# A sandwich layer on one core: where the expert mixing runs, how its chunks are paired, and where T4 is kept

## The chip, the cores and the metric

The kernel runs on one core of a Trainium2 chip. The metric is the device time of one execution in microseconds (us), the median of several runs. The core has a matrix engine (TensorE, PE in the profile, with its weight loads as PEld), VectorE (DVE), ScalarE (ACT), GpSimd (POOL) and SyncE (SP), whose queue issues all the DMA transfers of this kernel. Each engine takes its own instructions in the order in which the program emits them, and waits on semaphores for the others.

## The reference

Windowed attention with a residual, and then a feed-forward layer whose weights are mixed for each batch out of a base and eight experts, with a gate:

```python
x = x + layernorm(attention(layernorm(x), w_qkv))      # (4, 2048, 512), 16 heads, windows of 128
x = x + layernorm(ffn(layernorm(x), ...))

def ffn(hidden_states, ...):                            # (4, 2048, 512)
    h = relu(einsum('bsh,oh->bso', x, gate_w1) + gate_b1)
    g = (einsum('bso,eo->bse', h, gate_w2) + gate_b2).mean(axis=1)   # 8 numbers per batch
    mW1 = W1 + einsum('be,efh->bfh', g, TW1)            # 2048 x 512 per batch
    mb1 = b1 + g @ Tb1
    mW2 = W2 + einsum('be,ehf->bhf', g, TW2)            # 512 x 2048 per batch
    mb2 = b2 + g @ Tb2
    u = gelu(einsum('bsh,bfh->bsf', x, mW1) + mb1[:, None, :])
    return einsum('bsf,bhf->bsh', u, mW2) + mb2[:, None, :]
```

The gate's mean runs over a sequence's 2048 tokens, so each of the four sequences (the kernel's batches) has its own eight numbers and its own mixed weights. All is in float32.

## The kernel before

**Two phases.** First attention for all 64 windows, as a loop over 256 slots (`for i in range(NS)`, four slots to a window, one for each group of four heads). Into the slots lists of functions put the other work: norms, projections, the gate's products, the output. Then the feed-forward layer, as a loop over 16 blocks of 512 tokens (`for K in range(NBK)`), four blocks to a batch, so blocks 0 to 3 belong to batch 0 and blocks 8 to 11 to batch 2.

**Matrix products in Strassen's manner.** The products are cut into 2 x 2 quarters and done with seven products in place of eight (Winograd's form), for which sums of quarters of the left and the right factor are needed. The names A11, A12, S1 to S4, A22 are the seven left factors, T1 to T4 the sums of the right factor. For the second layer of batches 2 and 3 (`DEEP`, blocks 8 to 15) this is done twice, one inside the other: seven outer products (`o` from 0 to 6), each out of seven inner ones, with inner sums of the left factor (the weights) made once per batch and inner sums of the right factor (the activations) made by `inner_sums` for each block.

**A block.** Its first layer is four sets of two chunks (`for c in range(0, HC, 2)`), each of seven products: `begin` emits two, `middle` four, and the last one (A22, into the bank X) is emitted by `end` inside the next set's `middle`, or inside the second layer for the last set. In `middle` DVE adds Z into the tile `cpb` (L1145) and X into the tile `cpv` (L1148); the last product of the set writes X and so waits for L1148. Between its products `middle` calls `step()` four times, which advances the mixing. The second layer is `second` for batches 0 and 1 and `second_deep` for 2 and 3. Its weights come through `load_second`, from a list of all the tiles of all blocks (`coming`), into six buffers: six tiles are loaded ahead, and whenever PE has finished with a tile the next of the list is loaded. So the last tiles' places of a block take the first six of the next block.

**The mixing.** `mixer` is a generator over a list of jobs (`todo`). "mix" loads one expert's chunk (128 x 1024, 512 KB, into `exps`, four buffers) and adds it, times the gate's number, to `acc` on DVE (L251). A job can have two batches, and then one load serves two such additions. "sum" makes the three sums of a chunk and a difference (L262 to L265, in the tile `sums`, one buffer; on POOL while attention runs, then on DVE) and has the result stored into the weights' place in memory (`m1d`, `m2d`, `m3d`). "inner" loads two stored chunk pairs of batch 2, makes the inner sums (L117 to L120, on DVE) and stores them. Loads are three jobs ahead; stores are kept in `late` and issued by `flush` at the next job. A "mix" gives control back after each batch, an "inner" after each job, and a "sum" only in the feed-forward phase. For batch 3 the accumulators lie where the gate's weights were, so they can't begin until the gate is over, which is in block 0's second layer.

The list runs: batches 0 and 1 with both layers, chunk by chunk; chunks 0 to 3 of batch 2's first layer; the second layer of batches 2 and 3 in pairs; chunks 4 to 7 of the first layer in pairs, with inner sums of batch 2 behind each; chunks 0 to 3 of batch 3's first layer alone, with the rest of batch 2's inner sums. That is 416 expert loads and 512 additions. `MIXED` says how many steps each attention slot takes from slot 85 on (25 in 16 slots), `mixing(...)` how many are taken at each of the four calls in `middle` and after each of the seven products in `second`. The first list must have ended by block 8's second layer. The fourteen inner sums of batch 3 are a generator of their own (`inner_mixer`), stepped in block 9's first layer, with loads two ahead.

**T4 in the deep second layer.** T1 is used in the outer product 1, T3 in 3 (it lies in `top[..., Q:]`), T4 in 6. T4 is made by four subtractions on POOL (L1409), in T1's place, emitted in products 3 and 4.

Of the kernel before, what the change touches and what calls it, by code (L numbers as in the profile page):

```python
# [11 lines left out]
ALU = mybir.AluOpType  # L12
# [5 lines left out]
NB, L, D = 4, 2048, 512  # L18
# [6 lines left out]
NBLK = L // TB  # L25
# [9 lines left out]
def sandwich(ctx: ExitStack, tc: tile.TileContext, x, w_qkv, gw1, gb1, gw2, gb2, w1, b1, w2, b2, tw1, tb1, tw2, tb2, out):  # L35
# [72 lines left out]
    def load_inner(b, o, h):  # L108
        two = slice(2 * h, 2 * h + 2)
        et = mix.tile([P, 4, 2, P], F32, tag="exps", bufs=4, name=f"inner_{b}_{o}_{h}")  # L110
        nc.sync.dma_start(et[:, :2], m3_d[b][:, o, 0:8:7, two, :])
        nc.sync.dma_start(et[:, 2:], m3_d[b][:, o, 3:7:3, two, :])
        return et
# [12 lines left out]
        nc.sync.dma_start(m3_d[b][:, o, 4:6, two, :], et[:, 1:3])  # L126
        issued[b] += 1

    def inner_mixer(b):

        todo = [(b, o, h) for o in order_deep for h in range(2)]
        loaded, late = {n: load_inner(*todo[n]) for n in range(2)}, []
        yield
        for n in range(len(todo)):
            for f in late:
                f()
            if n + 2 < len(todo):
                loaded[n + 2] = load_inner(*todo[n + 2])
            et = loaded.pop(n)
            sum_inner(et)  # L140
            late = [lambda n=n, et=et: store_inner(*todo[n], et)]
            yield
        for f in late:
            f()

    attending, gated, gate_over = [True], set(), []

    def mixer():

        todo = []  # L150

# [9 lines left out]
                todo.append(("later", b, k, c))  # L161
            todo.extend(("inner", *x) for x in between)

        again = [(2, o, h) for o in order_deep for h in range(2)]
        for b in range(2):
            for k in range(2):
                for c in range(HC):
                    chunk((b,), k, c)
        for c in range(4):
            chunk((2,), 0, c)  # L170
        for c in range(HC):
            chunk((2, 3), 1, c)
        for c in range(4, HC):
            chunk((2, 3), 0, c, again[2 * c - 8 : 2 * c - 6])
        for c in range(4):
            chunk((3,), 0, c, again[2 * c + 8 : 2 * c + 10])
        assert not [x for x in todo if x[0] == "later"]

        loads = [x for x in todo if x[0] != "sum"]
        ets, accs = [], {}  # L180
        late = []

        def halves(t):
# [43 lines left out]
        def flush():  # L227
            for f in late:
                f()
            late.clear()  # L230
# [3 lines left out]
        yield  # L234
        for kind, *what in todo:
            if kind == "inner":
                load()
                flush()
                et = ets.pop(0)
                sum_inner(et)  # L240
                late.append(lambda what=what, et=et: store_inner(*what, et))
                yield
            elif kind == "mix":
                batches, s, c, e = what
                load()
                et = ets.pop(0)
                for b in batches:
                    flush()
                    assert b in gated
                    acc = accs[b, s, c]  # L250
                    nc.vector.scalar_tensor_tensor(acc, et, g_all[b][:, e : e + 1], acc, ALU.mult, ALU.add)  # L251
                    yield
            else:
                b, s, c = what
                flush()
                acc = accs.pop((b, s, c))
                q = [[acc[:, h, j * Q : (j + 1) * Q] for j in range(2)] for h in range(2)]

                a11, a12, a21, a22 = (q[i][j] if s == 0 else q[j][i] for i in range(2) for j in range(2))
                sums = mix.tile([P, 3, Q], F32, tag="sums", bufs=1, name=f"sums_{b}_{s}_{c}")  # L260
                engine = nc.gpsimd if attending[0] else nc.vector
                engine.tensor_tensor(sums[:, 0, :], a21, a22, ALU.add)  # L262
                engine.tensor_tensor(a21, a11, a21, ALU.subtract)
                engine.tensor_tensor(sums[:, 1, :], sums[:, 0, :], a11, ALU.subtract)
                engine.tensor_tensor(sums[:, 2, :], a12, sums[:, 1, :], ALU.subtract)  # L265
                late.append(lambda b=b, s=s, c=c, acc=acc, sums=sums: store(b, s, c, acc, sums))
                if not attending[0]:
                    yield
# [182 lines left out]
            us[c + side * HC] = wide[side][:, c // 2]  # L451

    us, wide = {}, {}
    blend = mixer()


    with ExitStack() as actx:
# [564 lines left out]
                f()  # L1022


        MIXED = (2, 1, 1, 2, 2, 1, 1, 2, 2, 1, 1, 2, 2, 2, 1, 2)
        for i in range(NS):
            W_, g = divmod(i, KC)
            nk = span_of(W_)[1]
# [39 lines left out]
    with ExitStack() as fctx:  # L1068
# [113 lines left out]
            (K, j, h) for K in range(NBK) for j in range(7) for h in range(4 if K // NBLK in DEEP else 2)  # L1182
        ]

        def load_second():

            if not coming:
                return
            K, j, h = coming.pop(0)
            b = K // NBLK  # L1190
            if b in DEEP:
                n = 2 if h < 3 else 1
                assert issued[b] > 2 * j + 1
# [108 lines left out]
        def second_deep(K, closing, load_x1):  # L1302
# [3 lines left out]
            if k == 0:  # L1306
# [10 lines left out]
                [top[..., Q:]],  # L1317
                t2,
                [bottom[..., Q:]],
                [t1],  # L1320
            ]
            Y = bank2("y2", f"py2_{K}")[:, 0, :P]
            part = lambda c, i, j: c[:, j, i * P : (i + 1) * P]
# [28 lines left out]
            for o in range(7):  # L1352
# [51 lines left out]
                emit((1, 1), Z)  # L1404
                if o < 6:
                    prepare(o + 1)
                if o in (3, 4):
                    for p in range(2 * o - 6, 2 * o - 4):
                        nc.gpsimd.tensor_tensor(t1[:, p], bottom[:, p, :, :Q], t2[p // 2][:, p % 2], ALU.subtract)  # L1409
                inner(2, X, summed(1))  # L1410
                emit((0, 1), X)
                if o:
# [139 lines left out]
        for K in range(NBK):  # L1552
            b, k = divmod(K, NBLK)
            if k == 0:
                mb2_of[b] = io.tile([P, D], F32, tag="mb2", bufs=1, name=f"mb2_{b}")
                nc.sync.dma_start(mb2_of[b], mb2_d[b])
            before = None
            for c in range(0, HC, 2):
                n = K * (HC // 2) + c // 2
                if n == 0:  # L1560

                    for cc in (0, HC):
                        for f in range(2):
                            bias = mb1_all[0][:, cc + f : cc + f + 1]
                            nc.scalar.activation(us[cc][:, f, :], us[cc][:, f, :], AF.Gelu_apprx_tanh, bias=bias)
                    hidden(2, 0, wts)
                    more_sums(0, 0)
                    for f in hooks[("set", 0)]:
                        f()
                    continue  # L1570
                S = begin(n)

                if n < 2:
                    step = mixing(0, 0, 0, 0)
                elif K == 0 or (k == NBLK - 1 and b + 1 < NB):
                    step = mixing(0, 1, 0, 1) if K == 0 else mixing(1, 1, 1, 1)
                else:
                    step = mixing(*((2, 1, 1, 1) if b == 0 or c > 2 else (1, 1, 1, 1)))
                if K == DEEP[0] * NBLK + 1:
                    if c == 0:  # L1580
                        assert next(blend, 0) == 0
                        inner = inner_mixer(NB - 1)
                    step = lambda: next(inner, None)
                middle(n, S, before, step)
                before = (n, S)

                for p in normed_y:
                    finish(*p)
                for p in normed_y:
                    if p[1] >= 2:  # L1590
                        load_x1(p[0], p[1] - 2)
                normed_y.clear()
                for p in pending[:2]:
                    standard(*p)
                    normed_y.append(p[:3])
                del pending[:2]
                for f in hooks.get(("set", n), ()):
                    f()
            if b in DEEP:
                if k == 0 and b == DEEP[0]:  # L1600
                    assert next(blend, 0) == 0
                products2 = second_deep(K, before, load_x1)
            else:
                products2 = second(K, before, mixing(3, 3, 3, 2, 3, 3, 2), load_x1)
            for j, _ in enumerate(products2):

                if j == (0 if K else 3) and K + 1 < NBK:
                    load_block(K + 1)
                if j == (2 if K else 5) and K + 1 < NBK and b not in DEEP:
                    for f in right_sums(K + 1):  # L1610
                        f()
                for f in hooks.get(("product", K, j), ()):
                    f()
# [56 lines left out]
```

## Time and profile before

| | |
|---|---|
| time, median of 3 runs | 3270.37 us (3268.0 to 3274.31) |
| the profiled execution | 3270.88 us, span 3269.1 us |
| mean granted TensorE clock | 0.994 |
| moved by DMA | 675.38 MB, mean 207 GB/s |
| DMA issues of `exps<-in_tw` | 416 of 512 KB, 5.5 us from issue to landing |
| additions L251 | 512, 717.5 us busy, mean 1416 ns |

The span is the time from the first to the last instruction; 1.8 us of the execution lie around it. Attention ends some 1700 us into the span, and a block of the feed-forward layer then takes 93 to 106 us. A busy share is the share of the time in which an engine had an instruction in work; the granted clock is what the throttle gave TensorE, 1.00 being full speed. A wait is shown as the instruction that waited, an arrow, and the instruction or transfer that released it.

### The profile page before, as it was taken

To read this page: it belongs to the slowest core of one execution; us is meant where nothing else is said; L and a number is where in the kernel's file an instruction comes from. 1 tells how busy PE (TensorE), PEld (TensorE's weight loads), DVE (VectorE), ACT (ScalarE), POOL (GpSimd) and SP (SyncE) were. 2 spreads that over 40 slices of the span, in tenths; PEclk is the share of its full clock that TensorE was granted. 3 is DMA by queue.
4 is the path that set the end of the run, shared out by engine and by line. 5 is a ranking of instruction groups with operands and counts; after the bars stand their busy time and mean duration, and the time that the engine had idled before them with its cause. 6 is when DMAs were issued, how large, how long until landed. Compare 5 with 4: busy or idle time off the path is not lost.

```text
span 3269.1 us, 63660 instructions
## 1 busy us (share of the span) xinstructions
PE 3204.8 (98%) x24534; PEld 2714.3 (83%) x24534; DVE 2275.9 (70%) x3309; ACT 1591.7 (49%) x4376; POOL 1067.4 (33%) x1162
## 2 busy tenths in 40 slices
PE   9999999999999999999999999999998989999998
PEld 7788878887778787878768888888887989999998
DVE  5655555889888889888865776777766674444555
ACT  3777777777677777777761222121221212322222
POOL 1222222343433445334332332333322323322323
PEclk9999999999999999999999999999999999999999
DMA  2111112566666667766787779878798784645555
GB/s 86 56 53 53 40 59 85 183 212 209 217 218 215 206 219 241 240 210 202 262 287 280 269 255 316 296 264 285 263 361 314 260 285 148 247 143 180 190 184 168
DMA packets 368319, 675.38 MB, mean 207 GB/s; under 512 B 28041, under 2 KB 137737, under 8 KB 362002
## 3 DMA queue, kind: packets, MB, share of 16 engines
q1 hardware_dynamic: 368018, 671.31, 60.2%
q8 instruction: 195, 3.19, 0.4%
q14 instruction: 106, 0.87, 0.1%
HBM read 546.42 MB, written 124.78 MB: 205 GB/s over the span
## 4 chain that ended last, share of the span: by engine, by line
PE 83%; DMA 7%; DVE 6%; issue 2%; POOL 2%; ACT 1%; SPq 1%; DVEq 0%; POOLq 0%; ACTq 0%
PE pm L581 20%; PE px L1088 12%; PE ptp L749 10%; PE sc L712 6%; PE pz L1088 6%; PE po L770 5%; PE px L1373 5%; PE px L1208 4%; PE pz L1208 3%; PE py L1088 3%; DMA exps<-in_tw 3%; PE pz L1373 2%; DMA fxT<-xTd 2%; DVE acc L251 1%; PE py L1208 1%
## 5 line engine op out<-in xcount | busy, mean ns | idle before, releaser
L251 DVE SCALAR_TENSOR_TENSOR acc<-exps,g,acc 128x1024 f32<-128x1024 f32 x512 | 717.5, 1416 | 50.2 <-DMA exps<-in_tw 46.0
L734 ACT ACTIVATE pr<-sc,nm 128x384 f32<-128x384 f32 (+1 forms) x1024 | 572.7, 589 | 41.3 <-DVE nm L721 41.2
L721 DVE TENSOR_REDUCE nm<-sc 128x2 f32<-128x768 f32 (+1 forms) x512 | 448.3, 916 | 165.3 <-PE sc L712 160.6
L754 ACT COPY prT<-ptp 128x512 f32<-128x512 f32 x732 | 383.4, 595 | 272.9 <-PE ptp L749 272.2
L749 PEld LDWEIGHTS ptp<-ident,pr 128*128 128x128 f32 x2944 | 317.8, 141 | 105.1 <-issue 90.7
L749 PE MATMUL ptp<-ident,pr 128*128 128x128 f32 x2944 | 379.5, 278 | 2.6 <-DVE g L855 2.2
L1088 PE MATMUL px<-tT,w 128*128 128x256 f32 x1512 | 355.1, 383 | 15.8 <-DVE cpv L1148 15.8
L1088 PEld LDWEIGHTS px<-tT,w 128*128 128x128 f32 x1512 | 289.3, 192 | 57.3 <-DVE cpv L1148 17.1
L1125 ACT COPY py<-px 128x512 f32<-128x512 f32 x63 | 36.0, 571 | 507.4 <-PE px L1088 507.4
L712 PE MATMUL sc<-k,q 32*128 32x384 f32 (+2 forms) x2816 | 251.4, 422 | 12.7 <-ACT pr L734 12.4
L1145 DVE TENSOR_TENSOR cpb<-pz,cpb 128x512 f32<-128x512 f32 x63 | 43.5, 690 | 312.8 <-PE pz L1088 252.5
L734 ACT ACTIVATION_READ_ACCUMULATOR pr<-sc,nm 128x1 f32 x1024 | 232.4, 227 | 0.0
L1170 POOL TENSOR_TENSOR t<-u 128x512 f32<-128x512 f32 x60 | 81.4, 1357 | 461.2 <-ACT u L1100 461.2
L96 POOL TENSOR_SCALAR ve_b<-mv_b 128x1 f32<-128x1 f32 x64 | 50.9, 795 | 553.3 <-DVE mv_b L94 553.3
L712 PEld LDWEIGHTS sc<-k,q 32*128 32x128 f32 x2816 | 122.5, 183 | 89.0 <-issue 51.6
L770 PEld LDWEIGHTS po<-prT,v 128*32 128x32 f32 x5888 | 152.2, 110 | 50.9 <-issue 27.7
L770 PE MATMUL po<-prT,v 128*32 128x128 f32 x5888 | 189.7, 275 | 0.2
L1373 PE MATMUL px<-w2s,inner_right 128*128 128x128 f32 x1344 | 178.9, 276 | 7.7 <-DVE y L1335 7.7
L581 PE MATMUL pm<-xnT,wqkv 128*128 128x256 f32 x720 | 172.0, 382 | 0.0
L1373 PEld LDWEIGHTS px<-w2s,inner_right 128*128 128x128 f32 x1344 | 163.9, 192 | 9.6 <-DVE y L1335 9.6
L1400 ACT COPY py<-px 128x128 f32<-128x128 f32 x56 | 14.0, 250 | 271.4 <-PE px L1373 182.9
L581 PEld LDWEIGHTS pm<-xnT,wqkv 128*128 128x128 f32 x720 | 132.0, 190 | 16.6
(303 smaller groups left out, 6334.4 us busy)
## 6 DMA issues: line engine op xcount, KB each, us to landing
exps<-in_tw SPq DMA_DIRECT2D x416, 512.0 KB, 5.5
w2s<-m3d SPq DMA_DIRECT2D x168, 512.0 KB, 4.7
w2s<-m2d SPq DMA_DIRECT2D x112, 512.0 KB, 6.3
acc<-in_w SPq DMA_DIRECT2D x64, 512.0 KB, 6.3
x<-in_x SPq DMA_DIRECT2D x64, 256.0 KB, 5.0
m1d<-acc SPq DMA_DIRECT2D x64, 256.0 KB, 6.4
w<-m1d SPq DMA_DIRECT2D x16, 1024.0 KB, 7.1
fxT<-xTd SPq DMA_DIRECT2D x16, 1024.0 KB, 7.4
```

The costliest lines, as they stand in the source:

```text
L251: nc.vector.scalar_tensor_tensor(acc, et, g_all[b][:, e : e + 1], acc, ALU.mult, ALU.add)
L581: nc.tensor.matmul(bank[u not in chain][:, half, :], lhsT=a[:, kc, ts(half, P)], rhs=b[:, kc, :], start=(u not in (2, 3, 4) and half == kc ...
L712: nc.tensor.matmul(scs[r // 2][:, r % 2, col : col + nj * W], lhsT=q[rows, g, ts(W_ % WB, W)], rhs=k_of[kb][rows, g, j0 * W : (j0 + nj) * ...
L721: nc.vector.tensor_reduce(st["nm"][:, h : h + 2], scs[u][:, :, : nk * W], AX.X, ALU.max, negate=True)
L734: nc.scalar.activation(pr[:, : nk * W], scs[r // 2][:, r % 2, : nk * W], AF.Exp, bias=st["nm"][:, h : h + 1], accum_out=st["den"][:, h : h ...
L749: nc.tensor.transpose(pt[:, r, :], st["pr"][g * 4 + r][:, ts(j, W)], ident)
L754: nc.scalar.copy(prT, pt)
L770: nc.tensor.matmul(po[r * E : (r + 1) * E, n, :], lhsT=v_of[kb][:, jj, h * E : (h + 1) * E], rhs=prT[:, r, :], start=(j == 0), stop=(j == ...
L1088: nc.tensor.matmul(bank[:, f, :], lhsT=factor[:, f, kc * P : (kc + 1) * P], rhs=right[:, kc, :], start=(start and f == 0 and kc == 0), sto ...
L1170: nc.gpsimd.tensor_tensor(t1s[c], b12, us[c][:, :, :Q], ALU.subtract)
L1208: nc.tensor.matmul(bank[:, t, :], lhsT=right(c - c % 2)[:, c % 2, ts(t, P)], rhs=w[:, c % (HC // 2), :], start=(start and c == 0 and t == ...
L1373: nc.tensor.matmul(bank, lhsT=right(p), rhs=w[:, p, :], start=(start and p == 0), stop=True, skip_group_check=True,)
```

## The change

The steps of the mixing are shared out differently, and five other things change with it.

- In attention `MIXED` takes 23 steps in 16 slots: slots 0, 1 and 13 of each 16 take one less, slot 14 takes one more.
- Pairing begins at chunk 2 of the first layer (chunks 0 and 1 of batch 2 alone, 2 to 7 for batches 2 and 3, then the whole second layer for both with half of batch 2's inner sums behind chunks 4, 5 and 6). The two chunks of batch 3 that are left become a list of their own. There are 400 expert loads.
- There are five lists. The first runs up to the end of block 7, and what is left of it is drained at the start of block 8. Block 8 takes the other half of batch 2's inner sums, block 9 chunks 0 and 1 of batch 3, blocks 10 and 11 seven inner sums of batch 3 each. Each list is started, with three loads, ahead of its block's first product. `inner_mixer` is gone.
- Per block, the calls of `middle` and `second` take other numbers of steps: two to a set in blocks 8, 10 and 11, five in block 9, 20 in a second layer of blocks 1 to 7 instead of 19, 21 in block 0.
- In an inner job and in a mix job `flush` comes ahead of `load`.
- `load_second` no longer loads tiles of the next block in a second layer. The first six tiles of a block are loaded in its own first layer, two ahead of each of the sets 2 to 4.
- T4 is written over T3 (`top[..., Q:]`), by the same four subtractions on POOL, emitted in the outer product 4.

```diff
-    def inner_mixer(b):
...
-    attending, gated, gate_over = [True], set(), []
-
-    def mixer():
+    attending, gated, gate_over, accs = [True], set(), [], {}
+
+    def mixing_plan():
...
-        again = [(2, o, h) for o in order_deep for h in range(2)]
         for b in range(2):
             for k in range(2):
                 for c in range(HC):
                     chunk((b,), k, c)
-        for c in range(4):
+        for c in range(2):
             chunk((2,), 0, c)
+        for c in range(2, HC):
+            chunk((2, 3), 0, c)
+        again = [(2, o, 0) for o in order_deep]
         for c in range(HC):
-            chunk((2, 3), 1, c)
-        for c in range(4, HC):
-            chunk((2, 3), 0, c, again[2 * c - 8 : 2 * c - 6])
-        for c in range(4):
-            chunk((3,), 0, c, again[2 * c + 8 : 2 * c + 10])
-        assert not [x for x in todo if x[0] == "later"]
+            chunk((2, 3), 1, c, {4: again[:3], 5: again[3:5], 6: again[5:]}.get(c, ()))
+        first = [("sum" if x[0] == "later" else x[0], *x[1:]) for x in todo]
+        todo.clear()
+        for c in range(2):
+            chunk((3,), 0, c)
+        second = [("inner", 2, o, 1) for o in order_deep]
+        third = [("inner", 3, o, h) for o in order_deep for h in range(2)]
+        return first, second, todo, third[:7], third[7:]
+
+    def mixer(todo):
...
             if kind == "inner":
+                flush()
                 load()
-                flush()
                 et = ets.pop(0)
                 sum_inner(et)
...
                 batches, s, c, e = what
+                flush()
                 load()
...
-    blend = mixer()
+    plans = mixing_plan()
+    blend = mixer(plans[0])
...
-        MIXED = (2, 1, 1, 2, 2, 1, 1, 2, 2, 1, 1, 2, 2, 2, 1, 2)
+        MIXED = (1, 0, 1, 2, 2, 1, 1, 2, 2, 1, 1, 2, 2, 1, 2, 2)
...
+        wanted = [0]
+
         def load_second():
 
-            if not coming:
+            if not coming or coming[0][0] > wanted[0]:
                 return
...
                 [bottom[..., Q:]],
-                [t1],
+                [top[..., Q:]],
             ]
...
-                if o in (3, 4):
-                    for p in range(2 * o - 6, 2 * o - 4):
-                        nc.gpsimd.tensor_tensor(t1[:, p], bottom[:, p, :, :Q], t2[p // 2][:, p % 2], ALU.subtract)
+                if o == 4:
+                    for p in range(PAIRS2):
+                        t3 = top[:, p, :, Q:]
+                        nc.gpsimd.tensor_tensor(t3, bottom[:, p, :, :Q], t2[p // 2][:, p % 2], ALU.subtract)
...
             before = None
+            if K >= DEEP[0] * NBLK and len(plans) > 1:
+                ending, blend = blend, mixer(plans[1])
+                plans = plans[:1] + plans[2:]
+                for _ in ending:
+                    pass
+                next(blend)
             for c in range(0, HC, 2):
+                if K and c:
+                    wanted[0] = K
+                    for _ in range(2):
+                        load_second()
...
                 elif K == 0 or (k == NBLK - 1 and b + 1 < NB):
-                    step = mixing(0, 1, 0, 1) if K == 0 else mixing(1, 1, 1, 1)
+                    step = mixing(1, 1, 1, 1)
                 else:
-                    step = mixing(*((2, 1, 1, 1) if b == 0 or c > 2 else (1, 1, 1, 1)))
-                if K == DEEP[0] * NBLK + 1:
-                    if c == 0:
-                        assert next(blend, 0) == 0
-                        inner = inner_mixer(NB - 1)
-                    step = lambda: next(inner, None)
+                    step = mixing(*((2, 1, 1, 1) if c == 2 or K == DEEP[0] * NBLK + 1 else (1, 1, 1, 1)))
+                if K >= DEEP[0] * NBLK and K != DEEP[0] * NBLK + 1:
+                    step = mixing(1, 0, 1, 0)
                 middle(n, S, before, step)
...
             if b in DEEP:
-                if k == 0 and b == DEEP[0]:
-                    assert next(blend, 0) == 0
+                assert next(blend, 0) == 0
                 products2 = second_deep(K, before, load_x1)
             else:
-                products2 = second(K, before, mixing(3, 3, 3, 2, 3, 3, 2), load_x1)
+                products2 = second(K, before, mixing(3, 3, 3, 3, 3, 3, 3 if K == 0 else 2), load_x1)
```

More of the change, by code (lines that the diff above doesn't have):

```diff
@@ L127, in store_inner @@
         issued[b] += 1
-    def inner_mixer(b):
[L131 to L144, printed above, removed]
-    attending, gated, gate_over = [True], set(), []
-    def mixer():
+    attending, gated, gate_over, accs = [True], set(), [], {}
+    def mixing_plan():
         todo = []
@@ L168, in mixer @@
                     chunk((b,), k, c)
-        for c in range(4):
+        for c in range(2):
             chunk((2,), 0, c)
+        for c in range(2, HC):
+            chunk((2, 3), 0, c)
+        again = [(2, o, 0) for o in order_deep]
         for c in range(HC):
-            chunk((2, 3), 1, c)
-        for c in range(4, HC):
-            chunk((2, 3), 0, c, again[2 * c - 8 : 2 * c - 6])
-        for c in range(4):
-            chunk((3,), 0, c, again[2 * c + 8 : 2 * c + 10])
-        assert not [x for x in todo if x[0] == "later"]
+            chunk((2, 3), 1, c, {4: again[:3], 5: again[3:5], 6: again[5:]}.get(c, ()))
[7 more added lines that the diff above has]
+    def mixer(todo):
         loads = [x for x in todo if x[0] != "sum"]
-        ets, accs = [], {}
+        ets = []
         late = []
```

## The prediction

> **What bounds the kernel now.** I read the page first, then the busy time by stretches (cut where each block's second layer begins), then the waits inside the bad stretches, then the timeline around single waits.
>
> ```profile
> span 3269.1 us, 63660 instructions
> PE 3204.8 (98%) x24534; PEld 2714.3 (83%) x24534; DVE 2275.9 (70%) x3309; ACT 1591.7 (49%) x4376; POOL 1067.4 (33%) x1162
> ```
>
> TensorE (PE) is busy 98% and the change takes no matmul away. So all that can be won is PE's 64 us without work, plus what PE loses at a lower granted clock. The stretches run from second layer to second layer: block 4 to 5, 6 to 8 (two blocks), 8 to 9, 9 to 10, 10 to 11. Columns: length, busy of PE, PEld, DVE, ACT, POOL, then granted clock, DMA share, GB/s.
>
> ```profile
> 2137.12:2233.81 96.69, 96.69 (x449) 85.12 (x449) 71.81 (x86) 22.69 (x48) 32.52 (x28) 1.00 0.78 262
> 2331.43:2543.40 211.97, 197.38 (x882) 170.32 (x881) 131.96 (x170) 42.81 (x92) 62.49 (x58) 0.97 0.86 313
> 2543.40:2637.97 94.57, 92.94 (x618) 86.47 (x617) 69.33 (x139) 24.98 (x59) 29.14 (x30) 1.00 0.88 290
> 2637.97:2743.84 105.87, 95.52 (x617) 88.86 (x616) 54.28 (x111) 25.17 (x59) 28.16 (x30) 0.95 0.53 184
> 2743.84:2837.20 93.36, 92.54 (x617) 86.48 (x616) 46.09 (x96) 24.98 (x59) 28.18 (x30) 1.00 0.67 230
> ```
>
> The first line is what an undisturbed shallow block takes (96.7), the last what a deep one takes (93.4). Blocks 6 to 8 cost 212.0 instead of 193.4, block 8 to 9 94.6 instead of 93.4, block 9 to 10 105.9 instead of 93.4: **18.6 + 1.2 + 12.5 = 32.3 us of excess**. Who is waited for, in 2331 to 2543 (total us, times, longest):
>
> ```profile
> PE py L1088 <- ACT py L1125: 6.2, 2, 4.4
> PE px L1088 <- DVE cpv L1148: 5.6, 1, 5.6
> DVE acc L251 <- DMA exps<-in_tw: 42.3, 22, 5.0
> ```
>
> DVE takes its instructions in order. A mix (L251) that waits for its expert weights holds the add L1148 behind it, and PE's last product of the set needs that add. The stretch loads 47 tiles for the mixing where two of the clean blocks load 34, since the chunks of batch 3 alone mix one batch for each 512 KB. Block 9's 9.5 us has another cause, in the timeline:
>
> ```profile
> 2647.81 0.68 DVE L1148 TENSOR_TENSOR cpv<-px,cpv 128x512 f32<-128x512 f32 x1
> 2648.55 3.78 PE L1088 MATMUL px<-tT,w 128*128 128x256 f32 x8 [9.53 <-DVE cpv L1148]
> ```
>
> Here it is inner sums that hold DVE: fourteen in one first layer, each load behind the store of an earlier one. After the wait eight matmuls take 3.78 instead of 1.89, so the excess is 9.5 of waiting and 3.0 of slow clock.
>
> The Trainium skill ("TensorE: Matmul & The Clock Gate", Part 1) says that an idle window of about 3.4 us halves PE's clock until PE has been busy for such a window again. By it a long wait costs some 1.7 us more; this trace's 3.0 is what I use. The rule speaks against the change wherever it leaves one new wait over 3.4 us.
>
> **Part by part.**
>
> *Loads rebalanced.* I counted the generator's steps slot by slot. Pairing from chunk 2 on takes 16 of 416 expert loads away. Before, blocks 1 to 7 load 18, 17, 15, 17, 19, 18, 31 tiles (expert and inner) and block 8 seven more. After, blocks 1 to 7 load 17, 17, 16, 16, 16, 20, 17. Block 4 of before, with 17, lost nothing, so blocks 6 and 7 should run clean: -18.6. Block 5's start of 0.9 over 96.7 (2233.81 to 2331.43) goes too: -0.9. Block 9's fourteen inner sums become seven each in blocks 10 and 11, two in a set of 12 us instead of four: -12.5. Block 8's second layer: -1.2. Sum **-33.2**.
>
> *Drain and restart at block 8.* The first plan ends with the last mix of block 7, and the sums of (2,1,7) and (3,1,7) are drained in one go ahead of block 8's first matmul. The tile of sums has one buffer, so the second sum waits on DVE until the stores of the first have landed; then SP issues its stores and only then the first inner loads; the first inner sum stands on DVE ahead of block 8's first adds, the second ahead of the first L1148. Times from block 8's first product (E): DVE ends the last adds, two mixes and statistics at E+5 (an undisturbed block end: 2086.88 to 2092.52 is 5.6 with a sum in place of a mix). First sum 4 x 0.42 = 1.7: E+6.9. Stores: six issues of 0.5; the last one that reads the sums lands 4.8 after its issue (2.5 for the quickest store near there): E+12 to 14. Second sum: E+14 to 16. Its stores and the first inner load, eight issues of 0.5, partly beside the sum: E+17.5 to 19. The load lands 5.0 later: E+22.5 to 24. Two inner sums and two adds, 2 x 1.7 + 2 x 0.68 = 4.8: L1148 ends at E+27 to 29. PE wants it after ten products of 1.73: E+17.3. Wait about 10, and with 3.0 of slow clock **+13** (5 if the landings are quicker and the loads pass SP early, 20 if they share the queues). The rows:
>
> ```profile
> m3d<-sums SPq DMA_DIRECT2D x32, 192.0 KB, 4.8
> inner<-m3d SPq DMA_DIRECT2D x56, 256.0 KB, 5.0
> exps<-in_tw SPq DMA_DIRECT2D x416, 512.0 KB, 5.5
> ```
>
> The last column is us from issue to landing.
>
> The skill ("DMA: Bandwidth & Descriptors", Anatomy of one DMA) fits a transfer, on another engine's path, with about 2.0 us plus its bytes by 436 GB/s, which makes an estimate of 2.5 for 192 KB and 2.6 for 256 KB. By it the chain would be some 4.7 us shorter and this term nearer +8; the landings in this trace are longer.
>
> *Chunks (3,0,0) and (3,0,1) in block 9's first layer.* Sixteen loads in 48 us, five to a set, and two second-layer loads: 7 x 0.52 MB in 12.1 us is 303 GB/s, between the clean 262 and the stretch at 313. Three loads are in flight, so 3 x 2.4 = 7.3 us for a landing of 5.5 (7.7 in the crowded stretch). At 5.5 nothing, at 7.7 some tenths a step: **+2** (0 to 10).
>
> *23 instead of 25 steps in 16 slots.* Slots 0, 1 and 13 lose one; these run beside POOL's right factors. What two mixes do there:
>
> ```profile
> 868.37 3.99 DVE L251 SCALAR_TENSOR_TENSOR acc<-exps,g,acc 128x1024 f32<-128x1024 f32 x2
> 869.15 2.13 POOL L546 TENSOR_TENSOR tx_False<-xnT,tx_False 128x512 f32<-128x512 f32 x1
> 872.28 1.27 DVE L721 TENSOR_REDUCE nm<-sc 128x2 f32<-128x512 f32 x2
> 874.13 0.70 PE L712 MATMUL sc<-k,q 32*128 32x256 f32 x4 [1.64 <-ACT pr L734]
> ```
>
> Two mixes take 3.99 instead of 2.56, the row maximum behind them is late, so are the exponentials and PE's next scores. PE waits 9.6 us this way from 590 to 1600, and the granted clock of 0.94 and 0.97 in two stretches of 50 us takes about 4. I take a third to a half of it: **-5** (-12 to 0).
>
> *Stores ahead of the load* (flush before load). While attention runs the sums are on POOL, and SP waits for them:
>
> ```profile
> SPq L213 <- POOL sums L264: 47.3, 7, 9.0
> SPq L224 <- POOL sums L265: 33.6, 6, 9.8
> ```
>
> Before, one expert load went ahead of that wait; now it stands behind. That load is needed four steps on, some 4 x 4.3 = 17 us, and lands 5.5 after its issue, so up to 11 us of waiting is covered, about what the longest 9.8 and the stores' 1.4 need. No gain is worked out for it: 0 (to +8).
>
> *T4 over T3.* The four POOL subtractions (L1409) now wait for PE's last read of T3, 5.4 us into product 3, instead of running during product 2.
>
> ```profile
> 2756.91 6.85 POOL L1409 TENSOR_TENSOR t<-u,t 128x512 f32<-128x512 f32 x4 [6.14 <-PE pz L1373]
> 2764.57 1.16 PE L1373 MATMUL px<-w2s,inner_right 128*128 128x128 f32 x8 [0.82 <-DVE y L1335]
> ```
>
> Beside them DVE's subtractions take 1.3 to 1.6 instead of 0.68, and PE waits 0.82 once in each deep block. In product 4 they meet four of the same subtractions. The result is read from product 5's third part on, some 2.7 us after they end. Wait moved, not removed: 0 (-6.5 if the eight waits go, +6.5 if they double).
>
> *Second-layer loads held back to the block's own first layer.* Six loads from the second set on, each with 12 us or more before its use against 4.7 to 6.3 to land, and six buffers as before: hidden by 36 us of first layer; without that cover about 6 us a block. It takes 3 MB out of each second layer. 0.
>
> *Block 0* gets four steps more in its sets and two in its second layer (six mixes, 8 us of DVE, busy 33 to 38 of 50 there), and loses six second-layer loads: **+1** (0 to 5).
>
> **Sum:** -33.2 + 13 + 2 - 5 + 1 = -22. The profiled execution took 3270.88 (span 3269.1 and 1.8 around it), 0.5 above the median 3270.37. So **3249 us**.
>
> **Rivals.** (1) *Block 8 starts clean*: the landings are quicker or the adds have more room, only some 3 us remain there. For it: stores of 2.5 us exist here. Against: three DMA legs in a row. -33.2 + 3 - 5 + 1 = -34: 3237. (2) *The excess only moves*: the starts of blocks 8 and 9 both cost 15 with their slow clock, attention wins nothing: -33.2 + 15 + 15 + 1 = -2, 3269, no change. For it: each plan is restarted cold with three loads. Against: blocks 9 to 11 wait for no store. (3) *Slower, by SP in attention*: the expert load behind POOL's sums comes late at the chunk ends, the mix holds the row maximum, and PE waits. There are about 30 sums in attention; at 2 us each that is +60 (with no clock loss), and 3249 + 60 = 3309; above 0.9 us a sum it decides. For it: 13 waits of SP of up to 9.8 us. Against: no mix waited for a load in attention before. (4) *The change doesn't relieve DMA*: the same mixes are done and only 8 of 675 MB saved. Then blocks 6 and 7 keep their 18.6: 3249 + 18.6 = 3268. Against: 31 loads against 17 in block 7.
>
> **How the numbers follow.** Main case 0.60; (1) 0.13; (2) and (4) 0.13; (3) 0.14. A measurement of this kernel can tell about 0.2% (6.5 us) from no change. Faster: the main case, (1) and a part of (2) and (4), 0.78; same 0.08; slower 0.14, which is (3). The main case alone spans 3236 to 3263; with (2) and (4) taken in the range is 3233 to 3272.
>
> **What would show it.** Blocks 6 and 7 at 96.7 between second layers and DMA waits of L251 gone there (else the first term is wrong). One PE wait of about 10 for L1148 some 17 us into block 8, with inner sums waiting for their loads before it; none in block 9. Second layers of blocks 10 and on 93.4 apart. POOL's L1409 in products 3 and 4, with the 0.8 wait behind it. In attention fewer than 9.6 us of waits by 1600. Wrong it would be with mixes waiting for loads in attention, or with waits of several us in every set of block 9.

## The result and the profile after

Run beside the kernel before on one chip, the changed kernel took 3292.53 us (3286.39 to 3294.88), the kernel before 3269.18: a ratio of **1.0067, 95% interval 1.0048 to 1.0086**. It is slower by 0.7%; 0.7% faster was forecast. The page of the changed kernel:

```profile
span 3293.1 us, 63613 instructions
PE 3214.6 (98%) x24534; PEld 2720.0 (83%) x24534; DVE 2278.7 (69%) x3321; ACT 1592.9 (48%) x4376; POOL 1015.6 (31%) x1150
```

Line numbers of the changed kernel and its variants are 7 to 10 lower than before: L1139 is L1148 of before, L1328 is L1335, L241 is L251. PE does the same 24534 matmuls. Its idle time grew from 64 to 78.5 us and its busy time by 9.8, about what the lower clock makes (mean 0.991 for 0.994, and 0.003 of the span is 9.9). Stretches from second layer to second layer, cut at the first product of each (blocks 6 to 8, 9 to 10, and now 11 to 12):

```profile
2352.54:2565.44 212.90, 199.51 (x898) 173.79 (x897) 141.07 (x187) 44.63 (x95) 61.56 (x59) 0.96 0.85 291
2659.90:2757.80 97.90, 94.71 (x617) 88.04 (x616) 64.88 (x129) 25.07 (x59) 29.22 (x31) 0.98 0.75 251
2850.82:2954.69 103.87, 96.26 (x618) 89.65 (x617) 47.71 (x96) 24.97 (x59) 26.96 (x30) 0.95 0.62 222
```

In the kernel before, blocks 6 to 8 cut at the same place:

```profile
2326.89:2543.40 216.51, 201.26 (x898) 173.44 (x897) 135.58 (x175) 43.89 (x95) 64.80 (x59) 0.97 0.84 307
```

The prediction's cut for block 6, 2331.43, lies 4.5 us behind that product, so its 212.0 is 4.5 too short. (Block 7 to 8 alone took 117.6 us before, so 93 to 106 us for a block does not hold for it.) Blocks 6 to 8 got 3.6 us faster (216.5 to 212.9), and block 9 to 10 got 8 back (105.9 to 97.9). Block 11 to 12, clean at 93.4 before, costs 103.9. From the timelines of the two, start of the second layers, in us:

| | before | after | difference |
|---|---|---|---|
| block 0 (so attention and block 0's first layer) | 1737.22 | 1759.40 | +22.2 |
| block 0 to 1 | 105.0 | 106.8 | +1.8 |
| 1 to 5 | 388.0 | 389.7 | +1.7 |
| 5 to 7 | 195.6 | 194.3 | -1.3 |
| 7 to 8 | 117.6 | 115.3 | -2.3 |
| 8 to 9, 10 to 11 | 187.9 | 187.5 | -0.4 |
| 9 to 10 | 105.9 | 97.9 | -8.0 |
| 11 to 12 | 93.4 | 103.9 | +10.5 |
| 12 to the end | 338.5 | 338.4 | -0.1 |

So 22 of the 24 us of span are lost before block 0's second layer begins, and the blocks behind it give back what they win and 2 us more. Of the 22, measured from 590 us on, 17 are PE's idle time (14.9 to 32.1 us) and 5 its busy time. Who waits in attention (590 to 1740 us; total, times, longest), first PE, then DVE:

```profile
PE sc L703 <- ACT pr L725: 10.1, 27, 1.3
PE ptp L740 <- DVE g L846: 6.1, 2, 3.8
PE ptx L392 <- DVE x L103: 5.6, 1, 5.6
PE ptx L392 <- DVE g L846: 3.8, 2, 3.1
```
```profile
DVE x L103 <- DMA x1d<-x: 50.9, 15, 7.2
DVE acc L241 <- DMA exps<-in_tw: 16.3, 7, 4.7
```

All of PE's waits over 1.3 us are for DVE. DVE itself stands 50.9 us (33.2 before) for the store of the residual: the second norm (`normed`, L103) writes `xn2` over `x1`, so it can't begin until the store of `x1` has landed. In 7 waits a mix stands for its load, which none did before. The longest case, SP, POOL, DVE and PE in order of time:

```profile
1702.48 0.73 POOL L255 TENSOR_TENSOR sums<-acc,sums 128x256 f32<-128x256 f32 x1
1703.24 0.37 SPq L213 DMA_DIRECT2D m2d<-sums  x1
1704.19 2.13 SPq L194 DMA_DIRECT2D exps<-in_tw  x3
1706.42 0.44 SPq L383 DMA_DIRECT2D x1d<-x  x1
1713.75 0.55 DVE L103 TENSOR_SCALAR x<-x,mv_c,rs_c 128x512 f32<-128x512 f32 x1 [7.20 <-DMA x1d<-x]
1714.44 1.09 PE L392 MATMUL ptx<-ident,x 128*128 128x128 f32 x4 [5.64 <-DVE x L103]
```

SP holds the stores until POOL has made the sums. The expert loads behind them go out three at once, 1.5 MB, and the residual's store is issued last. It lands 6.9 us after its issue (median of such stores 4.2; 3.2 before), and DVE and PE stand. Three loads is the extreme: of the 43 residual stores in this stretch 18 have one to three expert loads issued in the 3.5 us ahead of them, where before the change 7 had one or two. The Trainium skill ("DMA: Bandwidth & Descriptors", Queues, rings and completion order) says that a DMA engine consumes the descriptors of one issuer's ring in order. The 6.9 us behind three loads agree with that.

### The profile page after: what moved, and what is told of

Read it like the earlier page. It is cut to its first block, busy times and chain, and to the rows that moved or that the text cites. A ratio compares the mean times of both kernels' runs of the same rounds, so it can differ in the third digit from the quotient of the medians.

```text
span 3293.1 us, 63613 instructions
## 1 busy us (share of the span) xinstructions
PE 3214.6 (98%) x24534; PEld 2720.0 (83%) x24534; DVE 2278.7 (69%) x3321; ACT 1592.9 (48%) x4376; POOL 1015.6 (31%) x1150
## 4 chain that ended last, share of the span: by engine, by line
PE 84%; DVE 6%; DMA 5%; issue 2%; POOL 1%; ACT 1%; SPq 1%; DVEq 0%; POOLq 0%; ACTq 0%
PE pm L572 20%; PE px L1079 11%; PE ptp L740 10%; PE sc L703 6%; PE pz L1079 6%; PE px L1366 5%; PE po L761 5%; PE px L1201 4%; PE pz L1201 3%; PE py L1079 3%; PE pz L1366 2%; DVE inner_right L1291 2%; PE py2b L1201 1%; PE py L1201 1%; DMA x1d<-x 1%
## 5 line engine op out<-in xcount | busy, mean ns | idle before, releaser
L241 DVE SCALAR_TENSOR_TENSOR acc<-exps,g,acc 128x1024 f32<-128x1024 f32 x512 | 698.8, 1382 | 30.5 <-DMA exps<-in_tw 26.9
L703 PE MATMUL sc<-k,q 32*128 32x384 f32 (+2 forms) x2816 | 252.6, 423 | 12.1 <-ACT pr L725 11.9
L96 POOL TENSOR_SCALAR ve_b<-mv_b 128x1 f32<-128x1 f32 x64 | 40.6, 634 | 585.9 <-DVE mv_b L94 585.9
L761 PEld LDWEIGHTS po<-prT,v 128*32 128x32 f32 x5888 | 152.2, 110 | 50.9 <-issue 26.2
```

Source lines behind the costliest of these rows:

```text
L703: nc.tensor.matmul(scs[r // 2][:, r % 2, col : col + nj * W], lhsT=q[rows, g, ts(W_ % WB, W)], rhs=k_of[kb][rows, g, j0 * W : (j0 + nj) * ...
L761: nc.tensor.matmul(po[r * E : (r + 1) * E, n, :], lhsT=v_of[kb][:, jj, h * E : (h + 1) * E], rhs=prT[:, r, :], start=(j == 0), stop=(j == ...
```

## The experiments

Each ran beside the kernel before on the same chip. Block starts below are read off the timelines, like the table above.

**The order on SP alone.** `e1_load_first`, the changed kernel with

```diff
                 batches, s, c, e = what
-                flush()
                 load()
```

> The changed kernel with one thing undone: in a mix job the next load is issued ahead of the stores that wait, as before the change. The 23 steps in 16 slots stay. The time to block 0's second layer tells. Theory A (SP, held by stores that wait for POOL's sums, brings loads and the stores of the residual late, and so DVE): that start goes from 1759 back to 1737 to 1743 us, and the time from 3292 to 3270 to 3276. Theory B (the new table of steps does it, by where the steps fall): it stays at 1756 to 1760 and the time at 3290 to 3293.

Measured: block 0's second layer starts at 1735.87, the time is 3274.38 us, ratio 1.0008 (0.9999 to 1.0018).

`e2_before_flush_first`, the kernel before with

```diff
             if kind == "inner":
-                load()
                 flush()
+                load()
...
                 batches, s, c, e = what
+                flush()
                 load()
```

> The kernel before with one thing changed: the stores that wait are issued ahead of the next load, in mix and inner jobs. The 25 steps in 16 slots stay. Theory A: the start of block 0's second layer goes from 1737 to 1750 us or more, and the time from 3270 to 3283 or more. Theory B: it stays at 1737 and the time within 3 us of 3270.

Measured: 1755.62, 3286.07 us, ratio 1.0050 (1.0035 to 1.0065). Both ways round the order is worth 18.4 and 23.5 us up to that start, and the table of steps, with the order held, -1.4 and +3.8. The five later kernels with e1's attention start block 0's second layer at 1737.99 to 1742.54, so a start is not known to better than some 3 us: the table of steps changes nothing that shows. Theory A holds.

**How the order costs it.** `e10_own_xn2`, the changed kernel, order on SP as changed, with

```diff
-                **dict.fromkeys(("a", "x1", "xn2"), work.tile([P, D], F32, tag="x1", name=f"x1_{W_}")),
+                **dict.fromkeys(("a", "x1"), work.tile([P, D], F32, tag="x1", name=f"x1_{W_}")),
...
             }
+            win[W_]["xn2"] = win[W_]["xo"].rearrange("p k t -> p (k t)")
```

> The changed kernel with the second norm's result written into the tile that later takes its transposes, instead of over the residual; so DVE's L103 no longer waits until the store of the residual (x1d) has landed. The order on SP stays as changed. If attention loses its 22 us because the stores that wait for POOL's sums push three expert loads together in front of that store, and DVE stands for it (50.9 us of waits, 33.2 before), the start of block 0's second layer goes from 1759 to 1738 to 1745 us and the time from 3292 to 3271 to 3278. Rival (the mixes that wait for their loads themselves, 16.3 us in 7 waits, none before, hold DVE): it stays above 1752 and the time above 3285.

Measured: 1720.08, 3255.67 us, ratio 0.9954 (0.9937 to 0.9970). That is more than expected: the start is 39 us earlier than in the changed kernel and the time 37 lower. PE's largest and then DVE's wait for the loads there, in the same stretch:

```profile
PE sc L704 <- ACT pr L726: 3.3, 10, 0.7
```
```profile
DVE acc L241 <- DMA exps<-in_tw: 22.4, 13, 4.1
```

The mixes wait even longer for their loads, 22.4 us, and PE hardly minds: `e11` below has this edit among others, with the load first, only 2.3 us of such waits, and starts 1.6 us earlier. The rival falls: it is the wait for the residual's store that reaches PE. `e12_before_own_xn2` is the same edit on the kernel before.

> The kernel before with the second norm's result in the tile of its transposes, and nothing else. If the store of the residual is what DVE stands for in attention whatever the order on SP, and that order only sets how long, then here too the start of block 0's second layer goes to 1717 to 1722 us (1737 before), as in the changed kernel with the same edit (1720), and the time to 3249 to 3256. Rival (in the kernel before, the waits for that store, 33.2 us on DVE, are mostly covered, and 17 us of the gain of 39 came from the 23 steps): it stays above 1730.

Measured: 1713.36, 24 us earlier than without it, 3249.85 us, ratio 0.9938 (0.9921 to 0.9954). So the kernel before lost 24 us up to that start by that wait too (20 us of the time), and the changed kernel 39. Only 10 of the 24 are PE's idle time (14.9 to 4.5 us from 590 us on). In the other 13.5 PE was busy with the same matmuls, 8 of them in the scores' products, and why these go faster is not shown. With the wait gone the changed kernel's attention is still 7 us behind (1720 for 1713). Little of that is the order on SP, since `e11` starts at 1718; whether it is the table of steps is not settled.

**The second layer's held-back tiles.** `e3_hold_block8`, the changed kernel with

```diff
-            if not coming or coming[0][0] > wanted[0]:
+            if not coming or coming[0][0] == DEEP[0] * NBLK > wanted[0]:
...
-                if K and c:
+                if K == DEEP[0] * NBLK and c:
```

> The changed kernel with the second-layer tiles of a block loaded ahead in the block before it again; only those of block 8, whose weights aren't ready earlier, are held back. Theory C (the held-back loads are late in blocks 7 and 11, where the next batch's first-layer weights are loaded too): the waits for w2s of 5.5 us in block 7 and 6.8 us in block 11 go with their slow clock, blocks 7 to 8 take 106 to 108 instead of 115.3 and 11 to 12 takes 93.4 to 95 instead of 103.9, and the time falls by 14 to 19, to 3274 to 3278. Rival (the inner sums of batch 3 in block 11 hold SP, and so the first-layer weights come late and meet the second layer): block 11 to 12 stays at 100 or more, the time falls by less than 9.

Measured: 3289.82 us, ratio 1.0061 (1.0046 to 1.0076). Blocks 7 to 8 take 111.3 (115.3), 11 to 12 101.1 (103.9), and block 0 to 1 110.8 (106.8). Theory C falls as it was put: the hold alone is not the cause. The gain in blocks 7 to 8 can't be told from chance, because runs with the changed kernel's code there take 111.8 (`e4`) to 118.0 (`e10`). Here block 0 is 4 us slower without the hold; whether the hold spares it is taken up with `e8`. What stands in the way in block 11 of the changed kernel, SP's waits from 2833 to 2890 and the landing of the tiles from 2840 to 2880:

```profile
SPq L111 <- DMA m3d<-inner: 8.4, 2, 7.8
```
```profile
w2s<-m3d SPq DMA_DIRECT2D x9, 512.0 KB, 8.8
```

An inner load three jobs ahead takes the buffer whose store was issued just before it, and SP stands until that has landed; the next batch's first-layer weights and the tiles are behind it. `e5_inner_two_ahead` is e1 with

```diff
-        for _ in range(3):
+        for _ in range(2 if todo[0][0] == "inner" else 3):
             load()
```

> The changed kernel with the load ahead of the stores in a mix job, and the lists that begin with inner sums (blocks 8, 10, 11) loaded two jobs ahead instead of three, so that an inner load takes a buffer whose store was issued a job earlier. Beside the run with the load first alone (3274; block 11 to 12 103.7 us). Theory D (in block 11 SP stands before an inner load until the store just issued has landed, and the next batch's first-layer weights behind it come late and meet the second layer): block 11 to 12 falls from 103.7 to 97 or less, the time by 6 to 10, to 3264 to 3268. Rival (those weights, 7 MB, and the second layer's tiles are too much for DMA there in any order): block 11 to 12 stays above 101 and the time within 3 us of 3274.

Measured: block 11 to 12 100.6 (103.7), 3268.1 us, ratio 0.9993 (0.9984 to 1.0003). Between the two theories: 3 us of the 10 in that block. Only with both edits together most of it is gone, in `e7` below.

**The drain at block 8.** `e6_early_end` adds to e5

```diff
-                    step = mixing(*((2, 1, 1, 1) if c == 2 or K == DEEP[0] * NBLK + 1 else (1, 1, 1, 1)))
+                    step = mixing(*((2, 1, 1, 1) if c in (2, 4) or K == DEEP[0] * NBLK + 1 else (1, 1, 1, 1)))
```

> The run with two ahead, and one mixing step more in the third set of blocks 1, 2, 4, 5 and 6, so that the first list ends inside block 7's second layer and nothing is drained at block 8. If the drained sums are what makes block 8 start late (forecast: some 10 us of wait and 3 of slow clock), its wait of 7.2 for L1139 falls under 2 and block 7 to 8 goes from 110 to 97 to 100, the time by 9 to 13 against the run with two ahead. Rival (restarting a list cold costs it, whatever was drained): the wait stays above 5 and the time within 4 us.

Measured: block 7 to 8 100.8 for 109.7, and block 8's wait for L1139 is gone; PE's only wait left from block 7's second layer to block 8's:

```profile
PE px L1200 <- DMA w2s<-m2d: 2.2, 1, 2.2
```

So the drained sums make block 8 late, and not the restart. The time fell less than that, to 3265.59 us, ratio 0.9984 (0.9974 to 0.9994), since blocks 5 to 7 take 200.0 with the added steps (194.3 in `e5`). `e7_early_end_hold8` is e6 with e3's edit.

> The run with the early end, and second-layer tiles held back for block 8 alone. If the held-back loads still cost something in blocks 2, 3, 7 and 11 (0.8 each in 2 and 3), the time falls by 2 to 8 against the run with the early end. Rival (they spare block 0, which has the most transfers): block 0 to 1 grows by 2 to 4 and the time is the same or up to 3 us longer.

Measured: 3259.53 us, ratio 0.9967 (0.9956 to 0.9979). Block 7 to 8 takes 96.7 and 11 to 12 96.9 (clean 93.0). The time falls by 6, as expected, but block 0 to 1 takes 111.1 (106.8), as the rival said, and block 6 to 7 takes 103.4 (98.1).

**T4.** `e4_t4_back`, the changed kernel with

```diff
                 [bottom[..., Q:]],
-                [top[..., Q:]],
+                [t1],
...
-                if o == 4:
-                    for p in range(PAIRS2):
-                        t3 = top[:, p, :, Q:]
-                        nc.gpsimd.tensor_tensor(t3, bottom[:, p, :, :Q], t2[p // 2][:, p % 2], ALU.subtract)
+                if o in (3, 4):
+                    for p in range(2 * o - 6, 2 * o - 4):
+                        nc.gpsimd.tensor_tensor(t1[:, p], bottom[:, p, :, :Q], t2[p // 2][:, p % 2], ALU.subtract)
```

> The changed kernel with T4 written over T1 again, by two subtractions each in products 3 and 4. If the place of T4 is worth nothing, as forecast, the deep blocks 12 to 15 stay at 93.2 to 93.5 and the time within 3 us of 3292. Rival: the waits of 0.18 us behind the subtractions become 0.8 again, 8 x 0.6 = 5 us, and the time is 3297.

Measured: 3289.59 us, ratio 1.0058 (1.0043 to 1.0073), not to be told from the changed kernel. In the traces PE's waits behind L1328 are 7.8 us with T4 in T1's place and 3.6 in T3's, and a deep block takes 93.7 for 93.0 to 93.5. By the waits the place is worth some 4 us; the times don't show it.

**Putting the pieces together.** `e8_block0_as_before` is e7 with block 0 at two steps a set again, as in the kernel before, and added steps in three sets of blocks 1, 2 and 4, two of block 5 and one of block 6:

```diff
-                    step = mixing(1, 1, 1, 1)
+                    step = mixing(0, 1, 0, 1) if K == 0 else mixing(1, 1, 1, 1)
...
-                    step = mixing(*((2, 1, 1, 1) if c in (2, 4) or K == DEEP[0] * NBLK + 1 else (1, 1, 1, 1)))
+                    step = mixing(*((2, 1, 1, 1) if 2 <= c <= (6, 6, 6, 6, 6, 4, 2)[min(K, 6)] or K == DEEP[0] * NBLK + 1 else (1, 1, 1, 1)))
```

> The run with the early end and only block 8's tiles held back, with block 0's sets at two steps instead of four, as before the change, and no more steps in block 6 than the change gave it; blocks 1, 2, 4 and 5 take the steps instead. If block 0 is slow (111.1 against 105.0 before) for its four steps more, and blocks 5 to 7 (97.6 and 103.4) for the step added beside the inner sums, then 0 to 1 falls to 105 to 108 and 6 to 7 to 97 to 99, and the time to 3250 to 3255, below both kernels by 0.4% or more. Rival (block 0 is slow for the tiles of block 1 that it loads ahead; the steps don't matter): 0 to 1 stays at 110 or more.

`e9_hold1_and_8` is e8 with block 1's tiles held back too:

```diff
-            if not coming or coming[0][0] == DEEP[0] * NBLK > wanted[0]:
+            if not coming or (coming[0][0] in (1, DEEP[0] * NBLK) and coming[0][0] > wanted[0]):
...
-                if K == DEEP[0] * NBLK and c:
+                if K in (1, DEEP[0] * NBLK) and c:
```

> The same with the tiles of block 1 held back too, so that block 0 doesn't load them. If these loads are what makes block 0 slow, 0 to 1 is 3 to 5 us shorter than in the run beside it and the time too. If block 0's steps were it, both are within 1.5 us.

Measured: e8 3248.35 us, ratio 0.9928 (0.9913 to 0.9943), block 0 to 1 106.7, 6 to 7 96.7, 7 to 8 97.7; e9 3249.28 us, ratio 0.9930 (0.9917 to 0.9943), 0 to 1 106.4. Block 0 was slow by its four steps together with the tiles: 111.1 with both, 106.8 with the steps alone (`e6`), 106.7 with the tiles alone, 106.4 with neither. With the steps gone the tiles cost nothing. One trace each stands for this, and 106.8 and 108.3 came from the same code in that block (the changed kernel and `e10`). The time is a little below the 3250 to 3255 expected. `e11_block0_and_xn2` is e8 with e10's edit.

> The fastest run so far (load first, lists of inner sums two ahead, the first list ended in block 7, only block 8's tiles held back, block 0's sets at two steps) with the second norm's result in its own tile too. There L103's waits for x1d cost little (some 3 to 6 us of PE's waits), so the time falls by 0 to 6 from 3248. Rival: the waits only move to the next instruction on DVE, and it stays within 1.5 us.

Measured: **3224.07 us, ratio 0.9863 (0.9848 to 0.9877)**, 45 us below the kernel before; block 0's second layer starts at 1718.47 and the rest of the span takes 1508 us, 24 less than before. The edit is worth 22 us up to that start and 24 of the time here, about as in `e12`. The expected 0 to 6 counted PE's waits alone, and as in `e12` more than these goes away.

## Why the prediction was wrong, point by point

Forecast were -22 us, and the span grew by 24. Of the 46 us between, 27 lie ahead of block 0's second layer (-5 forecast, +22 measured) and 10.5 in block 11 to 12; the rest is spread over the other blocks.

**Stores ahead of the load: forecast 0 (to +8), measured some +20.** This is the step that failed. The rival on SP had the right place, the stores that wait for POOL's sums, and I gave it 0.14. But it named another path, a mix that comes late and holds the row maximum, so its slower time would have been near the result by luck. I asked whether the delayed load would still be in time for its mix. Some were not, 16.3 us in 7 waits, but for 22.4 us of such waits e10 and e11 show no more than 2 us. What I didn't ask is what else stands in SP's queue behind the held stores. It is the store of the residual, which now more often has loads issued just ahead of it. DVE's wait for it grew from 33.2 to 50.9 us, and with the order put back (e1) it is 30.7. The wait was in the trace of before, DVE's largest, and I took it for covered.

**23 steps: forecast -5, measured nothing that shows.** I read PE's waits in attention as pairs of mixes beside POOL. The timeline that I quoted begins just after a wait of DVE for that same store, which I left out:

```profile
867.30 0.55 DVE L103 TENSOR_SCALAR x<-x,mv_c,rs_c 128x512 f32<-128x512 f32 x1 [2.51 <-DMA x1d<-x]
```

DVE came 2.5 us late to the two mixes that hold the row maximum. With that wait taken away PE's waits in attention are 4 us (e12) with all 25 steps in place. So what the term was to save came mostly from that wait.

**Loads rebalanced: forecast -33.2, of which 12.5 - 4.5 came in blocks 9 to 10.** The counts were about right (block 7 issues 16 loads for the mixing, 29 before), and the second layers of blocks 1 to 7 begin 96.7 to 97.9 us apart. But the sum began from a wrong excess: by the cut at the first product, blocks 6 to 8 cost 23.1 too much and not 18.6, and block 5's 0.9 isn't there. Of the 23.1 only 3.6 came off. Block 7 to 8 keeps 18.6, some 10 of it the drain and 8.4 a late tile. The part for block 9 (fourteen inner sums shared out) holds. In the 4.5 left there a mix of batch 3's two chunks waits 4.3 us for its load and PE then 3.0 for L1139; forecast were +2.

**Drain at block 8: forecast +13, measured some +10.** The mechanism was right at each step:

```profile
2513.63 0.39 DVE L252 TENSOR_TENSOR sums<-acc 128x256 f32<-128x256 f32 x1
2515.30 0.37 SPq L209 DMA_DIRECT2D m3d<-sums  x1
2516.80 0.50 SPq L209 DMA_DIRECT2D m3d<-sums  x1
2519.10 0.42 DVE L252 TENSOR_TENSOR sums<-acc 128x256 f32<-128x256 f32 x1 [3.83 <-DMA m3d<-sums]
2523.39 0.50 SPq L111 DMA_DIRECT2D inner<-m3d  x1
2527.72 0.42 DVE L117 TENSOR_TENSOR inner<-inner 128x256 f32<-128x256 f32 x1 [6.93 <-DMA inner<-m3d]
2532.70 0.68 DVE L1139 TENSOR_TENSOR cpv<-px,cpv 128x512 f32<-128x512 f32 x1
2533.43 3.78 PE L1079 MATMUL px<-tT,w 128*128 128x256 f32 x8 [7.25 <-DVE cpv L1139]
```

First sum, its stores, the second sum that waits for them, the inner loads behind the second stores, two inner sums, L1139, and PE, which waited 7.25 (forecast 10). The two transfers took less: the last store that reads the sums (2516.80) lands 2.2 us after its issue and the load's second half (2523.94) 3.7, where I used 4.8 and 5.0. The skill's fit gives estimates of about 2.5 and 2.6 (in "DMA: Bandwidth & Descriptors", Anatomy of one DMA), near the store and 1.1 short for the load. After the wait eight matmuls take 3.78 us again, as in the kernel before.

**Held-back tiles: forecast 0; undone alone (e3), 3 us.** The sum left out the last block of each batch (7 and 11), where the next batch's first-layer weights (7 MB) go out in the same sets. There tiles came late, which costs some 19 us in the two blocks:

```profile
2475.04 0.90 SPq L1191 DMA_DIRECT2D w2s<-m2d  x2
2858.97 1.28 SPq L1188 DMA_DIRECT2D w2s<-m3d  x1
2485.15 9.95 PE L1201 MATMUL pz<-w2s,u 128*128 128x256 f32 x32 [5.48 <-DMA w2s<-m2d]
2870.36 2.05 PE L1366 MATMUL px<-w2s,inner_right 128*128 128x128 f32 x8 [6.84 <-DMA w2s<-m3d]
```

The first cost 5.5 and 2.9 of slow clock (9.95 for 7.07), the second makes most of block 11's 10.5. But neither tile is a held-back one. They are the ninth and the seventh tile of their blocks, issued in the second layer itself (the first two lines), and they land 10.0 and 11.3 us later. I had weighed the landing of one tile, 4.7 to 6.3 us, against 12 us of cover that these tiles never had. In e3, without the hold, block 11's seventh tile still goes out 5.7 us into the second layer (8.2 here), behind two loads of those weights, lands 11.9 us later, and PE waits 5.0. So I had priced the wrong loads: the six came in time, and those behind them were left out. The hold seems to make it a little worse. For block 11 the runs show that two things help, the hold undone and the inner loads two ahead (103.9 to 96.9 with both and the early end). That those weights are the rest of it is argued and not shown, since no run takes them away, and DMA is busy all the time there (382 GB/s from 2840 to 2880). How much each would cost by itself is not settled. Block 7's wait differs between runs with the same code there: block 7 to 8 took 115.3 in the changed kernel, 111.8 in e4 and 118.0 in e10.

**T4: forecast 0,** which holds within what the times can tell. **Block 0: forecast +1,** measured +1.8 (+3.3 in e10, with the same code there).

## What to carry to other kernels

When an instruction is moved ahead of another on an in-order DMA queue, list everything behind it up to the point where the queue is even again, small stores first, and ask of each who waits for its landing. An engine that overwrites a tile in place waits for the tile's last store; where a second tile that is free at that time can take the result, the queue's order all but stops mattering (here 24 to 39 us up to block 0's second layer for a change of two lines, which then begins at 1720 and 1718 us with the two orders). A wait that one engine shows and that "costs nothing" should be followed to the next late instruction before it is left out of the sum.

## What was not expected of the hardware

Fewer bytes did not mean faster transfers: the changed kernel moved 8.4 MB less, and its median landing of the residual's store in attention grew from 3.2 to 4.2 us, with more loads issued just ahead of it. And the feed-forward waits of 5.5, 6.8 and 7.3 us each cost PE some 3 us more by slow clock, like the one of 9.5 in the kernel before: for 5.9 us after the first (2485.15 to 2491) the granted clock was 0.50 to 0.58. So waits of this length cost about half as much again as they show.
